# One stream of score turns over all query blocks, with one extra turn per block for left keys and denominators

## The chip, the cores and the metric

The kernel runs on one core of a Trainium2 chip. The metric is the device time of one execution in microseconds (us). The kernel before was run three times: 3818.97 us median, 3816.32 to 3819.16.

## What is computed

The whole kernel is a chain of four layers over a tensor of 4 images, 56 x 56 pixels, 128 channels. Only the first layer matters here. It takes each image as 3136 tokens, applies attention in windows and then attention over all tokens of the image, and then a multilayer perceptron. The change is in the attention over all tokens, which is called once per image:

```python
q = (x @ wq + bq).reshape(n, s, NH, dk).transpose(0, 2, 1, 3)     # NH = 4 heads, dk = 32, s = 3136 tokens
...
scores = jnp.einsum('nhqd,nhkd->nhqk', q, k) / jnp.sqrt(jnp.float32(dk))
attn = jax.nn.softmax(scores, axis=-1)
out = jnp.einsum('nhqk,nhkd->nhqd', attn, v)
out = out.transpose(0, 2, 1, 3).reshape(n, s, c)
return out @ wo + bo
```

All data are 32-bit floats. The scores are small enough that no maximum is subtracted: the kernel takes exp of the scaled scores, sums the values with these weights, and divides by the sum of the weights.

## The kernel before

`fast_attention` (L572) first calls `fast_windows`, which leaves queries and keys transposed in `qT` and `kT` (128 partitions: 4 heads of 32 rows; 3136 columns) and the values in `va` (25 chunks of keys). The attention itself then runs over seven blocks `j` of 448 queries (NB = 448, NBLK = 7).

For one block the 3136 keys are 24 whole chunks `c` of 128 keys and 64 left keys (chunk 24). A **slot** is the score of one chunk and one head, 128 keys x 448 queries, and fills one bank of PSUM. So a block has 96 slots. Slots are handled in half turns. `bank(turn)` gives either four banks (`s0`) or three (`s1`), in alternation by the counter `n`; the eighth bank is `po`, in which the values add up. One half turn is up to four or three score matmuls on TensorE (PE; L661), and one exp on ScalarE (ACT; L663) that moves all these banks into consecutive slots of `ring` in SBUF. The ring has RING = 28 slots, seven chunks. A half turn is cut where the ring ends and where the block's 96 slots end (L657).

Three things read a chunk in the ring. `sums` (L603) adds chunks 0 to 21 into `acc` on VectorE (DVE; L606), 21 additions per block. `values` (L608) multiplies the chunk with the values into `po` (PE; L612), four matmuls, one per head. For chunks 22 and 23, which DVE does not add, `finish` multiplies by ones (L620), so that PE sums over keys; `acc` is multiplied by ones too, as the sum over the 128 partitions is still open.

After the 96 slots of a block comes a half turn for the left keys: scores (L673), exp into `p24` (L676). Work that reads exps is put into a list `late` with the turn from which it may run, and `flush` runs it after every second half turn. So values come some two half turns behind their exps, then `raw`, the copy of `po` to SBUF (L647, ACT), and then `finish` (L614): the denominators by ones into a bank (L620, L623), the output projection of the block before (L626), one copy of both to SBUF (L628, ACT), reciprocal (L629, DVE), product with `raw` (L630) and, for the block before, the addition to `xf` (L635). `finish` takes a half turn of its own. The last block's projection is L684.

The order on PE is that of the program (`manual_schedule`). The order on ACT and DVE in this stage is chosen by the scheduler of the language.

Of the kernel before, what the change touches and what calls it, by code (L numbers as in the profile page):

```python
# [12 lines left out]
F32 = mybir.dt.float32  # L13
AF = mybir.ActivationFunctionType
ALU = mybir.AluOpType
# [4 lines left out]
P = 128  # L20
B = 4
HH = 56
TOK = HH * HH
NB = 448
NBLK = TOK // NB
# [15 lines left out]
def blk(j):  # L41
    return slice(j * NB, (j + 1) * NB)
# [523 lines left out]


RING = 28
SUMMED = 22


def fast_attention(k, w, xw, xf, beside, mr):  # L572

    nc, tc = k.nc, k.tc
    scale = 1.0 / math.sqrt(32.0)
    heads = [slice(32 * h, 32 * h + 32) for h in range(4)]  # L580
    half = (slice(0, 64), slice(64, 128))
    with ExitStack() as es:
        big = es.enter_context(tc.tile_pool(name="f_big", bufs=1))
        qT = big.tile([P, TOK], F32, name="f_qT")
        kT = big.tile([P, TOK], F32, name="f_kT")
        va = big.tile([P, 25, P], F32, name="f_va")
        fast_windows(k, w, xw, xf, mr, beside, qT, kT, va)

        ring = es.enter_context(tc.tile_pool(name="f_ring", bufs=1)).tile([P, RING, NB], F32, name="f_ring")
        wk = es.enter_context(tc.tile_pool(name="f_wk", bufs=2))  # L590
        ps = es.enter_context(tc.tile_pool(name="f_ps", bufs=1, space=PSUM))
        oT = es.enter_context(tc.tile_pool(name="f_out", bufs=1)).tile([P, TOK], F32, name="f_oT")
        late = []
        n = 0

        def bank(turn):
            return ps.tile([P, (4, 3)[turn], 512], F32, tag="s%d" % turn, name="f_s%d" % turn)

        def slots(j, c):
            s = (96 * j + 4 * c) % RING  # L600
            return ring[:, s:s + 4, :]

        def sums(j, c, acc):  # L603

            if 0 < c < SUMMED:
                nc.vector.tensor_add(acc, slots(j, 0) if c == 1 else acc, slots(j, c))  # L606

        def values(j, c, po, p24):  # L608
            for h in range(4):
                o = half[h % 2] if c == 24 else slice(0, P)  # L610
                p = p24[o, h // 2, :] if c == 24 else slots(j, c)[:, h, :]
                nc.tensor.matmul(po[heads[h], :NB], va[o, c, heads[h]], p, start=(c == 0), stop=(c == 24))  # L612

        def finish(j, raw, acc, p24, pd):  # L614


            for c in range(SUMMED - 1, 24):
                p = acc if c < SUMMED else slots(j, c)
                for h in range(4):
                    nc.tensor.matmul(pd[heads[h], 0, :NB], k.ones[:, 0:32], p[:, h, :], start=(c < SUMMED), stop=False)  # L620
            for h in range(4):
                o = half[h % 2]
                nc.tensor.matmul(pd[heads[h], 0, :NB], k.ones[o, 0:32], p24[o, h // 2, :], start=False, stop=True)  # L623
            m = 1 + (j > 0)
            if j:
                nc.tensor.matmul(pd[:, 1, :NB], w.wo, oT[:, blk(j - 1)], start=True, stop=True)  # L626
            den = wk.tile([P, 2, NB], F32, name="f_den")
            nc.scalar.copy(den[:, :m], pd[:, :m, :NB])  # L628
            nc.vector.reciprocal(den[:, 0], den[:, 0])  # L629
            nc.vector.tensor_mul(oT[:, blk(j)], raw, den[:, 0])  # L630
# [6 lines left out]
        def flush(all_=False):  # L637

            nonlocal n
            if n % 2 and not all_:  # L640
                return
            while late and (all_ or late[0][0] < n):
                _, f, *a = late.pop(0)
                if f is finish:
                    a.append(bank(n % 2))
                    n += 1
                f(*a)  # L647

        with tc.manual_schedule(engines={mybir.EngineType.PE}):
            for j in range(NBLK):  # L650
                po = ps.tile([P, 512], F32, tag="po", name="f_po")
                raw = wk.tile([P, NB], F32, name="f_raw")
                acc = wk.tile([P, 4, NB], F32, name="f_acc")
                t, done = 0, 0
                while t < 96:
                    turn, slot = n % 2, (96 * j + t) % RING
                    m = min((4, 3)[turn], RING - slot, 96 - t)  # L657
                    ss = bank(turn)
                    for i in range(m):
                        c, h = divmod(t + i, 4)  # L660
                        nc.tensor.matmul(ss[:, i, :NB], kT[heads[h], c * P:(c + 1) * P], qT[heads[h], blk(j)],  # L661
                                         start=True, stop=True)
                    nc.scalar.activation(ring[:, slot:slot + m, :], ss[:, :m, :NB], AF.Exp, scale=scale)  # L663
                    t += m
                    while 4 * (done + 1) <= t:
                        sums(j, done, acc)
                        late.append((n + 2, values, j, done, po, None))
                        done += 1
                    n += 1
                    flush()  # L670
                ss = bank(n % 2)
                for h in range(4):
                    nc.tensor.matmul(ss[half[h % 2], h // 2, :NB], kT[heads[h], 24 * P:TOK], qT[heads[h], blk(j)],  # L673
                                     start=True, stop=True)
                p24 = wk.tile([P, 2, NB], F32, name="f_p24")
                nc.scalar.activation(p24, ss[:, 0:2, :NB], AF.Exp, scale=scale)  # L676
                late.append((n + 2, values, j, 24, po, p24))
                late.append((n + 2, nc.scalar.copy, raw, po[:, :NB]))
                late.append((n + 3, finish, j, raw, acc, p24))
                n += 1  # L680
                flush()
            flush(True)
# [1097 lines left out]
class Plan:  # L1780
# [655 lines left out]
def build(k, packs, I, out):  # L2436
# [3 lines left out]
    with ExitStack() as es:  # L2440
# [15 lines left out]
        with tc.tile_pool(name="w01", bufs=1) as wp, tc.tile_pool(name="io", bufs=1) as io:  # L2456
# [129 lines left out]
```

## Time and profile before

| what | before |
|---|---|
| median of three runs | 3818.97 us (3816.32 to 3819.16) |
| span of the profiled execution | 3813.2 us |
| the same, from first score to last projection, per image | 381.7, 381.7, 381.6, 382.8 us |
| PE busy in the span | 3506.3 us |
| DVE busy in the span | 2895.7 us |
| ACT busy in the span | 2076.4 us |
| exps of score slots (L663) | 796 |
| additions of chunks on DVE (L606) | 588 |

The profiled execution's own time is known by its span, from the first to the last instruction; the median of the runs is 5.8 us longer, which is what lies around the span. A busy time counts an engine once where instructions overlap. Each matmul of 32-bit floats has two records in the profile, so 2688 score matmuls appear as 5376. In a row of the timeline stand the start in us from the begin of the span, the length, the engine, the line, the operation, what is written and read, and in brackets the idle time of the engine ahead of it and what ended that.

### The profile page before, as it was taken

How to read it: one execution, taken by the hardware profiler on the slowest of the kernel's cores; microseconds unless marked ns; L12 is line 12 of the kernel's file. 1: busy time of each engine (PE TensorE's matmuls, PEld its weight loads, DVE VectorE, ACT ScalarE, POOL GpSimd, SP SyncE). 2: the span in 40 equal slices, each digit the busy share in tenths (PEclk: the TensorE clock that was granted, in tenths of full speed). 3: DMA queues.
4: the chain of work that ended last, by engine and by line, in shares of the span. 5: the costliest groups of instructions: out<-in, count | busy, mean ns of one | idle time of the engine just before them, and what ended most of it. 6: DMA issues, size and time to landing. Idle time of an engine off the chain costs nothing. (4 is left out here: it accounts for less than half of the span.)

```text
span 3813.2 us, 79448 instructions
## 1 busy us (share of the span) xinstructions
PE 3506.3 (92%) x35416; PEld 1559.0 (41%) x35416; DVE 2895.7 (76%) x2703; ACT 2076.4 (54%) x2080; POOL 1210.5 (32%) x667
## 2 busy tenths in 40 slices
PE   6899999989999898899999989998998889998998
PEld 4322234553222455322244552222456533335665
DVE  6588877858888787688878758888796666775676
ACT  4577765448777455577755448776553111213452
POOL 0000006600000372000016600000474768994677
PEclk8999999999999999999999999999998989999999
DMA  2000000000000000000000000000002036862011
GB/s 97 1 1 1 1 1 19 19 18 1 1 1 1 18 3 19 18 1 1 1 1 19 19 18 1 1 1 1 35 3 87 6 67 146 175 145 81 35 49 51
DMA packets 73497, 111.13 MB, mean 29 GB/s; under 512 B 62140, under 2 KB 63932, under 8 KB 67900
## 3 DMA queue, kind: packets, MB, share of 16 engines
q1 hardware_dynamic: 14460, 93.13, 8.2%
q10 hardware_dynamic: 58688, 12.85, 2.0%
q8 instruction: 280, 4.59, 0.5%
q14 instruction: 69, 0.57, 0.0%
HBM read 79.46 MB, written 26.51 MB: 28 GB/s over the span
## 5 line engine op out<-in xcount | busy, mean ns | idle before, releaser
L663 ACT ACTIVATE f_ring<-f_s 128x1792 f32<-128x1792 f32 (+3 forms) x796 | 1097.3, 1429 | 226.7 <-PE f_s L661 224.8
L606 DVE TENSOR_TENSOR f_acc<-f_acc,f_ring 128x1792 f32<-128x1792 f32 x560 | 1134.0, 2025 | 64.3 <-ACT f_ring L663 7.5
L661 PE MATMUL f_s<-f_qT,f_kT 32*128 32x448 f32 x5376 | 738.1, 571 | 48.0 <-ACT f_ring L663 29.0
L877 POOL TENSOR_TENSOR m_sq<-m_y 128x392 f32<-128x392 f32 x16 | 14.5, 919 | 1973.8 <-ACT m_y L876 1973.7
L612 PE MATMUL f_po<-f_ring,f_va 128*32 128x448 f32 x5376 | 589.7, 546 | 0.0
L1029 DVE TENSOR_TENSOR e_td<-e_pa,e_c 128x1792 f32<-128x1792 f32 x252 | 491.4, 2015 | 14.3 <-ACT e_a L994 14.3
L1031 POOL TENSOR_TENSOR e_tp<-e_a,e_c 128x1792 f32<-128x1792 f32 x140 | 451.8, 3259 | 145.2 <-PE e_acc L1036 104.4
L661 PEld LDWEIGHTS f_s<-f_qT,f_kT 32*128 32x128 f32 x5376 | 268.0, 183 | 525.0 <-ACT f_ring L663 379.3
L1036 PE MATMUL e_acc<-e_td,t_shared 32*32 32x448 f32 x8064 | 323.8, 546 | 22.3 <-DVE e_td L1029 11.2
L1033 ACT ACTIVATE e_tp<-e_tp 128x1792 f32<-128x1792 f32 x140 | 235.1, 1697 | 176.5 <-POOL e_tp L1031 176.5
L1645 DVE TENSOR_TENSOR u_ud<-u_px,u_d 112x1792 f32<-112x1792 f32 x144 | 240.1, 1708 | 96.4 <-PE u_po L1650 87.3
L612 PEld LDWEIGHTS f_po<-f_ring,f_va 128*32 128x32 f32 x5376 | 132.8, 108 | 396.7 <-issue 395.7
L1036 PE MATMUL e_acc<-e_tp,t_shared 32*32 32x448 f32 x4480 | 222.3, 547 | 3.2 <-ACT e_tp L1033 2.5
L1650 PE MATMUL u_po<-u_ud,AT 112*64 112x448 f32 x960 | 201.5, 549 | 23.4 <-DVE u_ud L1645 23.4
L1647 POOL TENSOR_TENSOR u_up<-xh,u_d 112x1792 f32<-112x1792 f32 x64 | 193.7, 3053 | 25.8 <-PE u_po L1650 12.4
L1036 PEld LDWEIGHTS e_acc<-e_td,t_shared 32*32 32x32 f32 x8064 | 134.0, 103 | 146.8 <-DVE e_td L1029 56.1
L629 DVE RECIPROCAL f_den<-f_den 128x448 f32<-128x448 f32 x28 | 82.7, 2953 | 77.2 <-ACT f_den L628 77.2
L1650 PE MATMUL u_po<-u_up,AT 112*64 112x448 f32 x576 | 127.0, 548 | 0.1
L1650 PEld LDWEIGHTS u_po<-u_ud,AT 112*64 112x64 f32 x960 | 64.9, 137 | 148.0 <-issue 86.7
L606 DVE TENSOR_TENSOR f_acc<-f_ring 128x1792 f32<-128x1792 f32 x28 | 56.7, 2024 | 86.6 <-ACT f_ring L663 57.8
L1512 POOL TENSOR_TENSOR q_u<-iS,q_g 128x1792 f32<-128x1792 f32 x32 | 102.8, 3236 | 55.8 <-PE s_px L1360 32.9
L1036 PEld LDWEIGHTS e_acc<-e_tp,t_shared 32*32 32x32 f32 x4480 | 95.1, 103 | 55.4 <-ACT e_tp L1033 19.3
(485 smaller groups left out, 4727.3 us busy)
## 6 DMA issues: line engine op xcount, KB each, us to landing
u_d<-dd SPq DMA_DIRECT2D x48, 784.0 KB
xw<-in_x SPq DMA_DIRECT2D x4, 1568.0 KB
x2d<-x SPq DMA_DIRECT2D x4, 1568.0 KB
xad<-x SPq DMA_DIRECT2D x4, 1568.0 KB
x_xs<-xad ACTq DMA_DIRECT2D x32, 196.0 KB
xm<-x_ev ACTq DMA_DIRECT2D x64, 98.0 KB
o_a<-xm SPq DMA_DIRECT2D x8, 784.0 KB
o_x<-x2d SPq DMA_DIRECT2D x4, 1568.0 KB
```

The lines of the kernel that those rows point to most:

```text
L606: nc.vector.tensor_add(acc, slots(j, 0) if c == 1 else acc, slots(j, c))
L612: nc.tensor.matmul(po[heads[h], :NB], va[o, c, heads[h]], p, start=(c == 0), stop=(c == 24))
L661: nc.tensor.matmul(ss[:, i, :NB], kT[heads[h], c * P:(c + 1) * P], qT[heads[h], blk(j)], start=True, stop=True)
L663: nc.scalar.activation(ring[:, slot:slot + m, :], ss[:, :m, :NB], AF.Exp, scale=scale)
L1029: nc.vector.tensor_tensor(t, am, cm, ALU.max)
L1031: nc.gpsimd.tensor_sub(t, bc(a.rearrange("p (l n) -> p l n", l=8), 1, 4), cm)
L1033: nc.scalar.activation(tf, tf, AF.Relu)
L1036: nc.tensor.matmul(acc[quarters[q], r, :NB], k.ident[o, o], t[o, q].rearrange("p l n -> p (l n)"), start=(g == 0), stop=(g == len(EDGE_TUR ...
L1512: nc.gpsimd.tensor_mul(u, bc(st.iS[:, bp, c, :HH], 1, HEADS), bc(g[:, n, c, :], 2, HH))
L1645: nc.vector.tensor_mul(u, bc(px[:, :, :NB], 2, m), dm)
L1647: nc.gpsimd.tensor_mul(u, bc(x, 2, m), dm)
L1650: nc.tensor.matmul(po[64 * b2:64 * b2 + 64, :NB], st.AT[:, 8 * i + h0 + q, 2 * bp + b2, :], u[:, b2, q, :], start=(left == 16), stop=(left ...
```

## The change

The score slots of all seven blocks become one stream of 672 slots in 96 turns. Every turn has a half turn of four slots and one of three; a turn may hold the end of one block and the begin of the next. `slots` stays as it was, since it already counted through the blocks. A list `queue` takes the chunks whose exps a turn has issued; `values()` runs what is in `ready` and then moves the queue there, so that values come one turn behind. It stops after a block's chunk 23, when `raw` is copied out of `po`, and leaves what follows for the next call.

The turn after a block's first slot (`ends`, with AFTER = 1: turns 0, 14, 28, 42, 55, 69 and 83) is followed by an extra turn: the left keys of the block that has just begun (`remainder`, in the four banks), a second call of `values()`, and the denominators of the block that has just ended (`finish`, in the three banks). The values of the left keys (chunk 24) come with the next turn's chunks, in the middle of the sum, and chunk 23 is the last.

ACT and DVE are issued in the order of the program in this stage too. DVE adds chunks 0 to 21 as before, and 0 to 20 in the last block, where PE takes 21 with 22 and 23. `BY_DMA` is empty, so the branches with a DMA are never taken.

```diff
-SUMMED = 22
+TURN = 7
+BY_DMA = ()
+BY_ONES = (22, 23)
+LAST_ONES = (21, 22, 23)
+AFTER = 1
...
+        def value(j, c):
+            e = blocks[j]
+            if c == 0:
+                e.po = ps.tile([P, 512], F32, tag="po", name="f_po")
             for h in range(4):
                 o = half[h % 2] if c == 24 else slice(0, P)
+                p = e.p24[o, h // 2, :] if c == 24 else slots(j, c)[:, h, :]
+                nc.tensor.matmul(e.po[heads[h], :NB], va[o, c, heads[h]], p, start=(c == 0), stop=(c == 23))
+            if c == 23:
+                e.raw = wk.tile([P, NB], F32, name="f_raw")
+                nc.scalar.copy(e.raw, e.po[:, :NB])
+
+        def values():
+
+            while ready:
+                j, c = ready.pop(0)
+                value(j, c)
+                if c == 23:
+                    break
+            ready.extend(queue)
+            queue.clear()
+
+        def remainder(j):
+            ss = bank(0)
+            for h in range(4):
+                nc.tensor.matmul(ss[half[h % 2], h // 2, :NB], kT[heads[h], 24 * P:TOK], qT[heads[h], blk(j)],
+                                 start=True, stop=True)
+            blocks[j].p24 = wk.tile([P, 2, NB], F32, name="f_p24")
+            nc.scalar.activation(blocks[j].p24, ss[:, 0:2, :NB], AF.Exp, scale=scale)
+
+        def finish(j):
+
+            e = blocks[j]
+            pd = bank(1)
+            for n, p in enumerate([e.acc] + [slots(j, c) for c in by_ones(j)]):
...
-        with tc.manual_schedule(engines={mybir.EngineType.PE}):
...
+        with tc.manual_schedule(engines={mybir.EngineType.PE, mybir.EngineType.Activation, mybir.EngineType.DVE}):
+            t = 0
+            ends = {-(-96 * j // TURN) - 1 + AFTER: j for j in range(NBLK)}
+            for turn in range(96 * NBLK // TURN):
+                for half_turn in range(2):
+                    m = (4, 3)[half_turn]
+                    ss = bank(half_turn)
                     for i in range(m):
+                        j, c = divmod((t + i) // 4, 24)
+                        h = (t + i) % 4
                         nc.tensor.matmul(ss[:, i, :NB], kT[heads[h], c * P:(c + 1) * P], qT[heads[h], blk(j)],
                                          start=True, stop=True)
+                    slot = t % RING
                     nc.scalar.activation(ring[:, slot:slot + m, :], ss[:, :m, :NB], AF.Exp, scale=scale)
+                    for q in range(t // 4, (t + m) // 4):
+                        queue.append(divmod(q, 24))
+                        add(*divmod(q, 24))
                     t += m
+                values()
+                if turn in ends:
+                    j = ends[turn]
+                    remainder(j)
+                    values()
+                    if j:
+                        finish(j - 1)
+                    queue.append((j, 24))
+            while ready or queue:
+                values()
+            finish(NBLK - 1)
```

In the rest of `finish` the matmuls by ones, the projection, the copy, the reciprocal, the product and the addition to `xf` are as before, with `e.p24` and `e.raw` in the places of `p24` and `raw`.

More of the change, by code (lines that the diff above doesn't have):

```diff
@@ L592, in fast_attention, with by_ones @@
         oT = es.enter_context(tc.tile_pool(name="f_out", bufs=1)).tile([P, TOK], F32, name="f_oT")
-        late = []
-        n = 0
+        blocks = [Env() for _ in range(NBLK)]
+        queue, ready = [], []
+        def by_ones(j):
+            return LAST_ONES if j == NBLK - 1 else BY_ONES
         def bank(turn):
@@ L601, in slots, with add @@
             return ring[:, s:s + 4, :]
[L603 to L608, printed above, removed]
+        def add(j, c):
+            e = blocks[j]
+            if c in by_ones(j):
+                return
+            if c in BY_DMA:
+                if c == BY_DMA[0]:
+                    e.far = wk.tile([P, 4, NB], F32, name="f_far", bufs=1)
+                    nc.sync.dma_start(e.far, slots(j, c))
+                else:
+                    nc.gpsimd.dma_start(e.far, slots(j, c), accum_op=ALU.add)
+                return
+            if c == 0:
+                return
+            if not hasattr(e, "acc"):
+                e.acc = wk.tile([P, 4, NB], F32, name="f_acc")
+                nc.vector.tensor_add(e.acc, slots(j, 0), slots(j, c))
+                return
+            if BY_DMA and c == last_add(j):
+                nc.vector.tensor_add(e.acc, e.acc, e.far)
+            nc.vector.tensor_add(e.acc, e.acc, slots(j, c))
@@ L609, in values, with last_add @@
+        def last_add(j):
+            return max(c for c in range(24) if c not in BY_DMA and c not in by_ones(j))
+        def value(j, c):
+            e = blocks[j]
+            if c == 0:
+                e.po = ps.tile([P, 512], F32, tag="po", name="f_po")
             for h in range(4):
                 o = half[h % 2] if c == 24 else slice(0, P)
-                p = p24[o, h // 2, :] if c == 24 else slots(j, c)[:, h, :]
-                nc.tensor.matmul(po[heads[h], :NB], va[o, c, heads[h]], p, start=(c == 0), stop=(c == 24))
@@ L614, in finish @@
-        def finish(j, raw, acc, p24, pd):
-            for c in range(SUMMED - 1, 24):
-                p = acc if c < SUMMED else slots(j, c)
+                p = e.p24[o, h // 2, :] if c == 24 else slots(j, c)[:, h, :]
[11 more added lines that the diff above has]
+            queue.clear()
@@ new lines, in remainder @@
+        def remainder(j):
[6 more added lines that the diff above has]
+        def finish(j):
+            e = blocks[j]
+            pd = bank(1)
+            for n, p in enumerate([e.acc] + [slots(j, c) for c in by_ones(j)]):
@@ L619, in finish @@
                 for h in range(4):
-                    nc.tensor.matmul(pd[heads[h], 0, :NB], k.ones[:, 0:32], p[:, h, :], start=(c < SUMMED), stop=False)
+                    nc.tensor.matmul(pd[heads[h], 0, :NB], k.ones[:, 0:32], p[:, h, :], start=(n == 0), stop=False)
             for h in range(4):
                 o = half[h % 2]
-                nc.tensor.matmul(pd[heads[h], 0, :NB], k.ones[o, 0:32], p24[o, h // 2, :], start=False, stop=True)
+                nc.tensor.matmul(pd[heads[h], 0, :NB], k.ones[o, 0:32], e.p24[o, h // 2, :], start=False, stop=True)
@@ L629, in finish @@
             nc.vector.reciprocal(den[:, 0], den[:, 0])
-            nc.vector.tensor_mul(oT[:, blk(j)], raw, den[:, 0])
+            nc.vector.tensor_mul(oT[:, blk(j)], e.raw, den[:, 0])
             if j:
@@ L635, in output @@
             nc.vector.scalar_tensor_tensor(xf[:, blk(j)], pm, w.fbvo, xf[:, blk(j)], ALU.add, ALU.add)
[L637 to L647, printed above, removed]
-        with tc.manual_schedule(engines={mybir.EngineType.PE}):
[L650 to L658, printed above, removed]
+        with tc.manual_schedule(engines={mybir.EngineType.PE, mybir.EngineType.Activation, mybir.EngineType.DVE}):
[5 more added lines that the diff above has]
+                    ss = bank(half_turn)
@@ L659, in fast_attention @@
                     for i in range(m):
-                        c, h = divmod(t + i, 4)
+                        j, c = divmod((t + i) // 4, 24)
+                        h = (t + i) % 4
                         nc.tensor.matmul(ss[:, i, :NB], kT[heads[h], c * P:(c + 1) * P], qT[heads[h], blk(j)],
                                          start=True, stop=True)
+                    slot = t % RING
                     nc.scalar.activation(ring[:, slot:slot + m, :], ss[:, :m, :NB], AF.Exp, scale=scale)
+                    for q in range(t // 4, (t + m) // 4):
+                        queue.append(divmod(q, 24))
+                        add(*divmod(q, 24))
@@ L664, in fast_attention @@
                     t += m
[L665 to L682, printed above, removed]
+                values()
[6 more added lines that the diff above has]
+                    queue.append((j, 24))
```

## Prediction

> **What bounds the kernel now.** The page comes first, for the engines and the groups that the change touches.
>
> ```profile
> PE 3506.3 (92%) x35416; PEld 1559.0 (41%) x35416; DVE 2895.7 (76%) x2703; ACT 2076.4 (54%) x2080; POOL 1210.5 (32%) x667
> ...
> L663 ACT ACTIVATE f_ring<-f_s 128x1792 f32<-128x1792 f32 (+3 forms) x796 | 1097.3, 1429 | 226.7 <-PE f_s L661 224.8
> L606 DVE TENSOR_TENSOR f_acc<-f_acc,f_ring 128x1792 f32<-128x1792 f32 x560 | 1134.0, 2025 | 64.3 <-ACT f_ring L663 7.5
> L661 PE MATMUL f_s<-f_qT,f_kT 32*128 32x448 f32 x5376 | 738.1, 571 | 48.0 <-ACT f_ring L663 29.0
> ```
>
> The second look is the busy table of four windows, each from an image's first score to its last projection (L684). The columns are window, length, then busy time of PE, PEld, DVE, ACT and POOL.
>
> ```profile
> 151.60:533.30 381.70, 360.88 (x3037) 110.64 (x3037) 324.88 (x167) 292.38 (x223) 0.00 (x0) 1.00 0.00 1
> 861.20:1242.90 381.70, 360.91 (x3037) 110.66 (x3037) 324.86 (x167) 292.42 (x223) 0.00 (x0) 1.00 0.00 1
> 1571.10:1952.70 381.60, 360.85 (x3036) 110.54 (x3036) 324.87 (x167) 292.39 (x223) 0.00 (x0) 1.00 0.00 1
> 2284.50:2667.30 382.80, 360.93 (x3036) 109.94 (x3036) 324.89 (x167) 292.64 (x223) 0.00 (x0) 1.00 0.00 1
> ```
>
> The stage takes 4 x 382 us, 40% of the span. PE is busy 361 of 382; DVE at 325 is second, ACT at 292 third. Third comes the timeline: one whole turn inside a block, then the turn of a block.
>
> ```profile
> 343.45 1.78 PE L661 MATMUL f_s<-f_qT,f_kT 32*128 32x448 f32 x14
> 344.55 2.85 ACT L663 ACTIVATE f_ring<-f_s 128x1792 f32<-128x1792 f32 x2 [0.94 <-PE f_s L661]
> 345.16 1.71 PE L612 MATMUL f_po<-f_ring,f_va 128*32 128x448 f32 x16
> ...
> 346.80 1.78 PE L661 MATMUL f_s<-f_qT,f_kT 32*128 32x448 f32 x14
> ...
> 356.74 0.98 PE L673 MATMUL f_s<-f_qT,f_kT 32*64 32x448 f32 x8
> ...
> 361.95 0.96 PE L612 MATMUL f_po<-f_p,f_va 64*32 64x448 f32 x8
> 363.07 0.96 PE L620 MATMUL f_s<-f_acc,c_ones 128*32 128x448 f32 x8 [0.17 <-ACT f_ring L663]
> ...
> 367.40 0.91 ACT L628 COPY f_den<-f_s 128x896 f32<-128x896 f32 x1 [3.52 <-PE f_s L626]
> 368.34 2.95 DVE L629 RECIPROCAL f_den<-f_den 128x448 f32<-128x448 f32 x1 [2.83 <-ACT f_den L628]
> ```
>
> Inside a block PE is back to back: seven score slots and two value chunks in 3.35 us, ACT waiting for PE. A turn with one value chunk is limited by the loop score, exp, score instead and takes 2.82 (at 336.85 and 339.67), the turn after it 3.78. Four turns hold seven chunks: 3.35 + 3.35 + 2.82 + 3.78 = 13.30 us, 3.325 a turn. A block of 96 slots is 96/7 = 13.71 turns, 45.6 us. The seven remainders (L673) of image 0 start at 198.56, 250.10, 303.67, 356.74, 410.88, 464.01 and 518.09: 53.26 us a block. So **7.66 us a block** go to the rest: the left keys, their values, the denominators, and turns cut short at the ring's end and the block's end.
>
> [...] I read PE from starts in the timeline, not from the 92%. [...] 14 records of 0.57 us on average end in 1.78 us, and rounds of four follow each other at 0.376 us. [...] the trace has 1.66 and 1.29, overlap 0.10. [...]
>
> **The change part by part.**
>
> *Turns.* Removed is the cut of turns. The ring of 28 is four times 7, so a stream of 4 and 3 never meets its end. Half turns per image before: 199 exps (796/4), 7 remainders, 7 denominators, 213. After: 192 + 14 = 206. The exps of L663 fall from 796 to 768. At a full half turn (1.67 us) this would be 7 x 1.67 = 11.7 us an image. But a short turn costs PE less than a full one, and the gain must be set against what the extra turn loses.
>
> *The extra turn.* I followed the new order, starting each piece when its engine is free and what it reads ended 0.055 us ago (the gap that the trace shows between an exp and the scores waiting for it); durations are those of the rows, with 0.54 for the copy of raw (L647), 0.92 for the left keys' exp (L676) and 0.91 for the denominators' copy (L628). Turn 28, from its first score: scores 0 and 0.86, exps 1.11 to 2.77 and 2.67 to 3.95, values of the old block's last chunk at 1.71. The remainder needs bank 0: 2.83. ACT copies raw behind both exps, 3.85 to 4.39, then exps the remainder until 5.20. The second call of values takes chunks 0 and 1, exps of this same turn; it needs the one accumulator bank and starts at 4.44, **PE standing 0.70**. Two chunks (1.64) bring 6.08. The denominators are 8 rounds of 0.376 plus 0.27 and the projection 0.95: 10.31. ACT's copy runs 10.47 to 11.37. Turn 29: four scores at 10.31, three must wait for bank 1 until 11.43, exps until 13.08 and 14.26; the list of values is empty. Turn 30: scores wait for these exps, 13.14 and 14.32; then three chunks (left keys, 2, 3) from 15.28 to 17.81. Three ordinary turns with five whole chunks take 3.35 + 2.82 + 3.78 = 9.95, so the extra turn costs **7.85 us**: 5.98 of its own PE work (0.91 + 0.84 + 4.23) and 1.87 of standing. The other five alignments give, from extra turn to extra turn, 53.7, 53.9, 51.8, 53.7 and 54.4 us for 69 turns: 267.5 - 69 x 3.325 = 38.1, **7.6 us a block**. Before it was 7.66.
>
> *DVE and ACT in program order.* The adds remain 21 a block (20 in an image's last block: 2.13 less for DVE there, 0.75 more for PE). DVE reaches the denominators' reciprocal at 5.3 and gets its input at 11.4, about 6 us idle; before it idled some 5 (2.83 for the copy, 1.8 ahead of the first add). It then follows 20 adds at 2.13 us, while chunks come every 1.90: it falls behind, and PE's finish finds the sum ready by 1.1 to 3.1 us. Ring slots come free 4 us before they are needed. Both are hidden by these margins, nothing else. Nothing in the stage runs on POOL or a DMA queue that is moved.
>
> *Ends.* Lead-in: turn 0 has a remainder too, and turn 14 starts at 49.9 (14 x 3.325 = 46.6, and 3.3 of filling and first table load). Then 267.5. From turn 83 to the final projection 64.2: 47.8 to turn 95 (17.8 for the extra turn's three, then nine of 3.33), and from there DVE's last add (6.8), finish with one more chunk (5.1), copy, reciprocal and product (4.5). Total **381.5 us an image**. The same rule on the old order gives 382.3 where the trace has 381.7. The difference by one rule is -0.7, against the trace itself -0.1; times four, -0.5 to -3 us. I take -3: the profile's 3813.2 goes to 3810. The span is 5.8 below the median of the runs, which holds what lies around it: 3819.0 - 3 = **3816**. The 28 extra turns each have waits that no trace shows; at +-0.3 us each that is +-8, so 3808 to 3825 for this case.
>
> **The rivals.** About 0.2% (7.6 us) is what a measurement can tell from no change.
>
> *The bubbles close* (0.18). If the extra turn costs only its 5.98 us, each of 24 interior blocks gains 1.7 and the stage 41: 3778. For it: seven half turns fewer per image, ACT free for 90 us of each. Against: the one accumulator bank, and two turns with 0 and 3 chunks in place of 2 and 2, come from the order itself.
>
> *DVE takes over* (0.22), the case on the slower side. Place: the first matmul of finish, which waits for the last add. It decides from 1.1 us of lateness at the tightest block on. Twenty adds at 2.23 instead of 2.13 would be 2 us late; with 1.5 us of it seen by PE in 24 blocks, 36 us: 3852. For it: DVE idles a microsecond longer per block, in fixed order behind the reciprocal. Against: adds measure 2.025 and start 2.13 apart with no wait, and the page counts only 7.5 us of waiting for exps.
>
> *The change does not do what it says*: turns still cut. Excluded by 28 = 4 x 7; the count of L663 would show it.
>
> *No change* (0.60) is the forecast: two orders with the same rounds, the same adds, and 7.6 against 7.66 us of loss. Range: to leave out no more than 2 in 10, half of each rival: 3793 to 3842; the likeliest case alone 3808 to 3825. Faster 0.18, same 0.60, slower 0.22.
>
> **What would show it.** L663's exps 768, in two forms of 384; ordinary turns still 3.35 us; about 10.3 us from the extra turn's first score to the next turn's, then 2.8 and 4.7; extra turns 51.8 to 54.4 us apart; stage 381 to 382. PE waiting for L606 at the denominators in every block would be the DVE rival; extra turns 51.5 us apart on average the fast one. If the extra turn's three windows differ from 17.8 by over a microsecond, my prediction is wrong in its main step.

## Result and profile after

The kernel after took 3829.23 us (median of six runs, 3826.52 to 3830.47), beside 3817.64 us for the kernel before in runs of the same time (3814.45 to 3819.25): ratio 1.0026, 95% interval 1.0015 to 1.0038. It is slower by 11.6 us. The forecast was 3816, no change. The profiled spans are 3827.2 us after and 3813.2 before, 14.0 apart. A run's time exceeds its span by 1.7 to 2.1 us in every execution on record. So of the 5.8 us that were taken for what lies around the span, some 4 are that the profiled execution of before was faster than the median; and the 14.0 are a little more than the medians differ.

First the same parts of the page as before: the engines, the exps, the additions, the scores. The last line is the reciprocal of the denominators; the figure behind its last bar is DVE's idle time ahead of it.

```profile
PE 3493.9 (91%) x35448; PEld 1560.1 (41%) x35448; DVE 2892.5 (76%) x2699; ACT 2069.8 (54%) x2052; POOL 1209.3 (32%) x667
...
L701 ACT ACTIVATE f_ring<-f_s 128x1792 f32<-128x1792 f32 (+1 forms) x768 | 1091.2, 1475 | 193.9 <-PE f_s L698 191.0
L630 DVE TENSOR_TENSOR f_acc<-f_acc,f_ring 128x1792 f32<-128x1792 f32 x556 | 1125.7, 2025 | 56.8 <-ACT f_ring L701 1.4
L698 PE MATMUL f_s<-f_qT,f_kT 32*128 32x448 f32 x5376 | 718.2, 571 | 54.7 <-ACT f_ring L701 28.2
...
L680 DVE RECIPROCAL f_den<-f_den 128x448 f32<-128x448 f32 x28 | 82.7, 2953 | 138.8 <-ACT f_den L679 138.8
```

The change does what it says: 768 exps in two forms instead of 796 in four, 556 + 28 additions instead of 588, and 32 records of matmuls more (one chunk more by ones in each image's last block: 4 images x 4 heads x 2 records). DVE waits 62 us more ahead of its 28 reciprocals (138.8, before 77.2), 2.2 us each.

Then the busy table, one window per image from its first score to its last projection (now L718), the columns as before:

```profile
151.00:531.80 380.80, 356.03 (x3045) 110.14 (x3045) 322.94 (x166) 290.54 (x216) 0.00 (x0) 1.00 0.00 1
860.00:1240.80 380.80, 356.07 (x3045) 110.13 (x3045) 322.89 (x166) 290.54 (x216) 0.00 (x0) 1.00 0.00 1
1569.60:1953.60 384.00, 358.98 (x3044) 110.48 (x3045) 322.93 (x166) 290.61 (x216) 0.00 (x0) 0.99 0.00 1
2283.60:2665.40 381.80, 356.10 (x3045) 108.92 (x3045) 322.92 (x166) 291.07 (x216) 0.00 (x0) 1.00 0.00 1
```

The attention did not become slower. Three of four images take 0.9 to 1.1 us less than before. The last projection starts at 2665.40; before it started at 2667.34. At that point the kernel after is 1.9 us ahead. From there to the end of the span it needs 3827.2 - 2665.4 = **1161.8 us**, the kernel before 3813.2 - 2667.3 = **1145.9 us**. The loss of 15.9 us lies in code that the diff does not touch, and so not in the first layer, which alone was said to matter here.

Going on in the timeline of after, TensorE first. These are its rows in the spectra of the second layer, some 220 us after the last projection:

```profile
2883.02 6.69 PE L1356 MATMUL s_pr<-t_images,s_x 128*64 128x33 f32 x223 [1.00 <-DVE x L1043]
2892.81 0.19 PE L1356 MATMUL s_pr<-t_images,s_x 128*64 128x33 f32 x1 [3.10 <-issue]
...
2906.03 1.83 PE L1394 MATMUL s_px<-t_images,s_z 128*112 128x112 f32 x16
2924.20 0.58 PE L1284 MATMUL s_pt<-s_mv,t_shared 128*128 128x1 f32 x2 [16.34 <-DVE s_mv L1281]
```

The same rows of before:

```profile
2884.76 6.73 PE L1322 MATMUL s_pr<-t_images,s_x 128*64 128x33 f32 x224 [1.05 <-DVE x L1009]
...
2903.04 1.83 PE L1360 MATMUL s_px<-t_images,s_z 128*112 128x112 f32 x16
2908.02 0.38 PE L1250 MATMUL s_pt<-s_mv,t_shared 128*128 128x1 f32 x2 [3.16 <-DVE s_mv L1247]
```

Two waits are new. In the first transform PE does 223 of 224 records of matmuls and stands 3.10 us ahead of the last, for nothing that the profile shows ("issue"). Later it waits 16.34 us for `s_mv` from DVE, where it waited 3.16. Measured from the last projection, the matmul with `s_mv` comes at 258.8 us after and 240.7 us before, 18.1 later; 15.9 of that is left at the end. Behind its waits PE is also slower. Over the 20 us from the transform's first matmul the granted clock, as a share of TensorE's full clock, was 0.91 (before 1.00), and over the next 40 us 0.61 (before 0.74). How much of the 15.9 us that makes was not separated.

What DVE does meanwhile, in the timeline of after, with POOL's rows at the two moments that count:

```profile
2907.42 0.87 DVE L1784 TENSOR_TENSOR t_w_M<-t_w_M,t_w_M0rev 112x1 f32<-112x1 f32 x1
2907.65 1.40 POOL L1438 TENSOR_SCALAR d_m<-t_w_V,t_images 128x448 f32<-128x448 f32 x1
2908.99 3.82 DVE L1785 TENSOR_TENSOR t_w_M<-t_w_M,t_w_M0rev 112x1 f32<-112x1 f32 x1
2912.73 11.39 DVE L1787 TENSOR_SCALAR t_w_M<-t_w_M 112x62 f32<-112x62 f32 x1
...
2922.95 1.12 POOL L1451 TENSOR_TENSOR d_d<-d_d,d_t 128x448 f32<-128x448 f32 x1
2924.16 1.70 POOL L1450 TENSOR_SCALAR d_t<-t_w_V,t_images 128x448 f32<-128x448 f32 x1
```

And of before:

```profile
2904.43 0.14 DVE L1750 TENSOR_TENSOR t_w_M<-t_w_M,t_w_M0rev 112x1 f32<-112x1 f32 x1
2905.69 0.60 DVE L1751 TENSOR_TENSOR t_w_M<-t_w_M,t_w_M0rev 112x1 f32<-112x1 f32 x1
2906.21 0.18 DVE L1753 TENSOR_SCALAR t_w_M<-t_w_M 112x62 f32<-112x62 f32 x1
...
2908.28 1.40 POOL L1404 TENSOR_SCALAR d_m<-t_w_V,t_images 128x448 f32<-128x448 f32 x1
```

The three operations are small steps on weights of the third layer (`conv_weights`). They take 0.14, 0.60 and 0.18 us before, and 0.87, 3.82 and 11.39 after. On DVE the statistics `s_mv` stand right behind them. In before they end 1.9 us ahead of the large POOL operation `d_m` (2906.39 to 2908.28). In after DVE reaches them 4.9 us later, counted from the last projection, and meets POOL's run of large operations of `value_weights` and `score_weights`. In before DVE meets that run too, with later operations, and eleven of them take half a microsecond or more longer than alone. But they take only 0.9 to 1.5 us each, and none overlaps more than two instructions of POOL. That run has 17 POOL instructions in the 11.39 us, and its first pause is from 2924.07 to 2924.16. DVE's operation ends at 2924.12, in that pause. The hold of 3.82 us ended without a pause of POOL.

So the theory has two steps. **First**, PE's instructions come in packets, and where one packet ends has moved. The page's queue table has 280 instruction packets of 4.59 MB in all on queue q8, 16.4 KB each. PE has 71,238 records in the trace: 35,448 of matmuls, as many of weight loads, and 342 of its sequencer. If q8 carries PE's instructions, that is 254 records a packet. That it does is inferred, and the author's estimate for a packet is 256, which is also how far apart the two records lie at which PE waits in the runs below (58,112 and 58,368). Counting PE's records from 0 at the start of the trace, the matmul that waited is number 58,368 = 228 x 256. In the kernel before, that number falls 40 records behind the transform's last, and PE, which first waits 0.73 us for DVE there, shows no wait for its instructions. The change makes it 40 records earlier: 64 more of matmuls and weights, 24 fewer of the sequencer. **Second**, the delay puts DVE's small operations in step with POOL's run, which holds them.

The rivals: that the new order of attention leaves something behind (DVE or a transfer later than before); and that POOL's run is no cause, but a thing that stands beside it.

### The profile page after: what moved, and what is told of

It reads as the page before. It is cut to its first block, busy times and chain, and to the rows that moved or that the text cites. A ratio compares the mean times of both kernels' runs of the same rounds, so it can differ in the third digit from the quotient of the medians.

```text
span 3827.2 us, 79464 instructions
## 1 busy us (share of the span) xinstructions
PE 3493.9 (91%) x35448; PEld 1560.1 (41%) x35448; DVE 2892.5 (76%) x2699; ACT 2069.8 (54%) x2052; POOL 1209.3 (32%) x667
## 3 DMA queue, kind: packets, MB, share of 16 engines
q8 instruction: 280, 4.59, 0.5%
## 5 line engine op out<-in xcount | busy, mean ns | idle before, releaser
L701 ACT ACTIVATE f_ring<-f_s 128x1792 f32<-128x1792 f32 (+1 forms) x768 | 1091.2, 1475 | 193.9 <-PE f_s L698 191.0
L698 PE MATMUL f_s<-f_qT,f_kT 32*128 32x448 f32 x5376 | 718.2, 571 | 54.7 <-ACT f_ring L701 28.2
L698 PEld LDWEIGHTS f_s<-f_qT,f_kT 32*128 32x128 f32 x5376 | 258.6, 183 | 520.5 <-ACT f_ring L701 387.6
L680 DVE RECIPROCAL f_den<-f_den 128x448 f32<-128x448 f32 x28 | 82.7, 2953 | 138.8 <-ACT f_den L679 138.8
L1546 POOL TENSOR_TENSOR q_u<-iS,q_g 128x1792 f32<-128x1792 f32 x32 | 102.8, 3239 | 72.5 <-PE s_px L1394 49.9
L891 ACT ACTIVATE m_hT<-m_ph,w_fb 128x392 f32<-128x392 f32 x128 | 72.8, 589 | 70.3 <-PE m_ph L890 64.9
```

## Experiments

The table collects all runs. "Rest" is the profiled time from the last projection to the end of the span. Rest, waits and hold are each of one profiled execution. Each ratio is to the kernel before in runs of the same time, whose medians were 3817.64 us (beside after), 3820.05 (the runs with 10 and 54 matmuls, `t_w_M` on POOL, one call), 3820.50 (the late weights with `d_`, and one call + 47) and 3821.43 (the runs without `d_`, and + 64 matmuls); so medians of different lines compare to some 4 us only. "PE waits" are the waits of over 0.5 us without a shown cause in the first transform of the spectra or just behind it; "hold" is the longest of DVE's operations on single columns or weights of up to 384 elements there, which take 0.1 to 0.4 us when nothing holds them.

| kernel | median us | ratio to before, 95% | rest us | PE waits us | hold us |
|---|---|---|---|---|---|
| before | 3817.64 | | 1145.9 | none | 1.23 |
| after | 3829.23 | 1.0026 (1.0015 to 1.0038) | 1161.8 | 3.10 | 11.39 |
| before + 10 matmuls | 3829.28 | 1.0025 (1.0016 to 1.0033) | 1160.8 | 2.44 | 11.38 |
| before + 64 matmuls | 3819.11 | 0.9997 (0.9988 to 1.0005) | 1146.1 | none | 1.24 |
| after + 54 matmuls | 3819.17 | 0.9995 (0.9987 to 1.0003) | 1146.8 | none | 1.63 |
| after, `t_w_M` on POOL | 3824.87 | 1.0010 (1.0004 to 1.0017) | 1157.1 | 3.12 | 7.94 |
| after, conv weights late | 3829.89 | 1.0026 (1.0016 to 1.0036) | 1165.5 | 2.52 | 3.96 |
| after, without `d_` operations | 3820.85 | 1.0001 (0.9992 to 1.0009) | 1155.1 | 3.98, 1.35 | 0.35 |
| one call | 3790.34 | 0.9924 (0.9911 to 0.9936) | 1160.5 | 0.71, 2.84 | 7.07 |
| one call, late | 3789.60 | 0.9921 (0.9908 to 0.9935) | 1160.3 | 1.47 | 4.50 |
| one call + 47 matmuls | 3772.19 | 0.9879 (0.9864 to 0.9894) | 1145.4 | none | 1.23 |
| the same, late | 3792.66 | 0.9925 (0.9911 to 0.9938) | 1160.3 | none | 7.73 |
| the same, late, without `d_` | 3787.96 | 0.9913 (0.9900 to 0.9927) | 1156.1 | 3.16, 3.04 | 0.22; 3.15 at the weights' new place |

The rest takes one of two sizes, 1145 to 1147 or 1155 to 1166, whatever the attention is.

### The packet's end alone, in the kernel before

Ten matmuls of one column (two records of matmul and two of weights each, so 40 records) ahead of the last image's final projection. The attention is the old one.

```diff
+PADS = [0, 0, 0, 10]
...
-        pm = ps.tile([P, 512], F32, tag="po", name="f_pf")
+            pm = ps.tile([P, 512], F32, tag="po", name="f_pf")
+            for _ in range(PADS.pop(0)):
+                nc.tensor.matmul(pm[0:32, 500:501], k.ones[:, 0:32], oT[:, 0:1], start=True, stop=True)
```

> The kernel before, with ten one-column matmuls (40 records on PE) ahead of the last image's final projection, where PE waits about 5 us for DVE anyway. They write a column of PSUM that nobody reads. Theory A (where PE's instruction stream is cut): in the changed kernel PE has issued 41 records more than before when the spectra begin (57922 against 57881), and there PE stands 3.1 us ahead of the last matmul of L1356 with nothing to wait for but its own instructions; DVE then meets POOL's run of additions and is held some 15 us. With 40 records more the kernel before has the cut at the same place: PE stands about 3 us there, and the run takes about 3828 to 3832, that is 10 to 14 us more than before. Theory B (the order on ACT and DVE, or the data's place, is the cause): 3818, unchanged within 3 us.

The kernel before, with 0.9 us of work added on PE, takes 3829.28 us, 9.2 more than the kernel before beside it: by the ratios the same loss. (The first transform starts at record 57,922 in after and 57,882 in before, 40 apart, not the 41 of the expectation.) The timeline of this kernel, PE and DVE:

```profile
2898.86 2.19 PE L1341 MATMUL s_ps<-s_z,t_images 128*128 128x56 f32 x6 [2.44 <-issue]
...
2918.59 11.38 DVE L1756 TENSOR_SCALAR t_w_M<-t_w_M 112x62 f32<-112x62 f32 x1
```

The wait stands just behind the transform, at record 58,369, one from the multiple of 256, and the same operation is held as long as in after. The new attention is not needed for the loss.

### A whole packet more, in the kernel before

The same edit with 16 matmuls per image: 64, or 256 records, the estimate for a packet.

```diff
+PADS = [16, 16, 16, 16]
```

> The kernel before with 64 one-column matmuls (16 ahead of each image's final projection), 256 records of PE more[...], so the cuts between packets fall where they fell before. The theory (where the cut falls decides) expects no wait of 2 us in the first transform or the inverse transform, the operations on t_w_M under 1 us, and no more than the matmuls' own time: 3818 to 3825. The rival, that more instructions on PE are late as such, expects more than ten matmuls gave: 3829 or above, with PE's wait of 2 to 3 us.

3819.11 us, no difference, with over six times as many matmuls added as in the run that lost 9 us. PE waits nowhere in the transform, the holds are those of before. More instructions as such cost nothing here; what matters is where the multiples of 256 fall. This was not varied finely: the kernels without `d_` aside, PE waits where the transform starts 65 to 90 records behind a multiple, and does not where it starts 18 to 26 behind.

### The packet's end put back, in the kernel after

```diff
+PADS = [14, 14, 13, 13]
```

> The changed kernel, with 54 one-column matmuls (216 records on PE) spread as 14, 14, 13, 13 over the waits ahead of the four final projections. 41 + 216 = 257[...], so the cuts of PE's stream stand in the spectra as they do in the kernel before. Theory A: PE's wait of 3.1 us ahead of the last matmul of the first transform is gone, DVE isn't held for 11 us at t_w_M, and the run takes 3812 to 3818, some 13 us less than the changed kernel's 3829. Theory B: 3829 and more, up to 4 us for the matmuls where they stick out of the wait.

The 257 of the expectation is one more than the 256 records estimated for a packet. The run took 3819.17 us, ratio 0.9995: the loss is gone, by adding work. The timeline has 224 matmuls without a wait, and DVE passes:

```profile
2888.65 6.73 PE L1359 MATMUL s_pr<-t_images,s_x 128*64 128x33 f32 x224 [1.00 <-DVE x L1046]
...
2909.61 1.63 DVE L1788 TENSOR_TENSOR t_w_M<-t_w_M,t_w_M0rev 112x1 f32<-112x1 f32 x1
2911.16 0.18 DVE L1790 TENSOR_SCALAR t_w_M<-t_w_M 112x62 f32<-112x62 f32 x1
```

With the rest as it was, the change is what the prediction said of it, no change.

### The held operations taken from DVE

The operations on `t_w_M` go to POOL.

```diff
-        nc.vector.tensor_add(m[:, 0, 0:1], m[:, 0, 0:1], rev[:, 0:1])
-        nc.vector.tensor_sub(m[:, 1, 0:1], m[:, 1, 0:1], rev[:, 1:2])
-        nc.vector.tensor_scalar_mul(m[:, :, 0], m[:, :, 0], 0.5)
-        nc.vector.tensor_scalar_mul(m[:, :, 1:], m[:, :, 1:], math.sqrt(2.0))
+        nc.gpsimd.tensor_add(m[:, 0, 0:1], m[:, 0, 0:1], rev[:, 0:1])
+        nc.gpsimd.tensor_sub(m[:, 1, 0:1], m[:, 1, 0:1], rev[:, 1:2])
+        nc.gpsimd.tensor_scalar_mul(m[:, :, 0], m[:, :, 0], 0.5)
+        nc.gpsimd.tensor_scalar_mul(m[:, :, 1:], m[:, :, 1:], math.sqrt(2.0))
```

> The changed kernel, with the eight small operations of conv_weights on t_w_M issued on POOL instead of DVE. Theory A: what costs most is DVE held behind POOL at three of these operations (0.9 + 3.8 + 11.4 us where before they took 0.9 in all). On POOL they can't be held by POOL: 3815 to 3820, 9 to 14 us less than the changed kernel; PE's wait of 3.1 us at the first transform stays. Rival C (DVE is held by whatever operation comes there[...]): the additions, squares and factors behind them are held instead, 3825 to 3829.

3824.87 us, between the theory and its rival: some 4 us of the 12 by the medians, 6 by the ratios, and 4.7 in the rest. DVE's next weights take the place of those moved (timeline of this kernel):

```profile
2909.00 4.30 DVE L1789 TENSOR_SCALAR t_w_W<-t_w_W 128x384 f32<-128x384 f32 x1
...
2914.01 7.94 DVE L1791 TENSOR_SCALAR Wr<-t_w_W 128x384 f32<-128x384 f32 x1
```

So it is not the operation itself that is slow: what comes in its place at that time is held.

In another kernel all of these weights (`conv_weights`, except what needs the slot pool) are issued at the end of `spectra`, behind the statistics.

```diff
+        conv_weights(k, w, st.conv)
...
-def conv_weights(k, w, pool, late):
+def conv_weights(k, w, pool):
...
+def conv_slots(k, w, pool, late):
```

> The changed kernel, with all of conv_weights but its last tile (slot) issued on DVE at the end of the spectra, behind their last copies, instead of in their middle, where POOL adds without a pause. PE's instructions are as in the changed kernel, so its wait of 3.1 us at the first transform stays. Theory A (the first loss is PE's wait, the larger one DVE held behind POOL at these operations): DVE reaches the aggregate (s_mv) without being held, 10 to 13 us come back and up to 3 go for the operations at their new place: 3817 to 3822. Rival C (whatever comes on DVE is held as long): 3826 to 3830.

No gain, 3829.89 us, as the rival had it. `s_mv` itself is free (1.67 us at 2909.37), but the next operation on single columns, `s_t` at L1289, is held 3.96 us, `s_d` at L1300 2.60, and at their new place several of the moved weights are held some 3 us each. Of the expected gain 6.3 us come, and go again. The last `s_px` matmul (L1394) ahead of the matmuls on `q_u` is that much sooner than in after, counted from the last projection (311.2 us, 317.5). Then the first matmul on `q_u`, which DVE makes behind these weights, waits 12.14 us where it waited 3.3.

### POOL's run taken away

```diff
-    half = wk.tile([32, 2, HH], F32, name="d_half")
...
     f = wk.tile([P, 3, 8, HH], F32, name="d_f")
-    for ri in range(2):
-        nc.gpsimd.tensor_scalar_mul(t, w.V[:, ri], w.pvh[:, 0:1])
...
+    nc.gpsimd.memset(f, 0.0)
```

> The changed kernel with the products and sums of value_weights (d_half to d_f, 18 operations on POOL) left out: d_f is set to zero, so the second layer's values are left out of what it computes. What the same engine does beside it, the q_ operations of score_weights, stays. If DVE is held by POOL's gapless run (theory), that run ends some 10 us earlier: PE still stands 3 us in the first transform, since nothing changes for its instruction packets, but the DVE operation that took 11.39 us takes under 4, s_mv comes some 10 us sooner, and the time is 3814 to 3821. If DVE was held by something else that comes with PE's wait (its own instructions late, a transfer), taking POOL's work away changes only what waits for POOL: 3826 to 3831, and the operation still takes over 8 us.

3820.85 us, inside the theory's range, ratio 1.0001. (Seventeen operations are left out, not 18.) In the timeline the same operation of 112x62 takes 0.19 us, and no weight takes over 0.35:

```profile
2906.51 0.35 DVE L1771 TENSOR_SCALAR Wr<-t_w_W 128x384 f32<-128x384 f32 x1
2906.78 0.16 DVE L1766 TENSOR_SCALAR t_w_M<-t_w_M 112x2 f32<-112x2 f32 x1
2906.84 0.19 DVE L1767 TENSOR_SCALAR t_w_M<-t_w_M 112x62 f32<-112x62 f32 x1
```

POOL's other operations there, the `q_` ones, now end at 2897.67, where in after they run to 2922.97, and DVE's small ones come in another order. So the edit moved more than it took away. What it shows is that with POOL idle nothing on DVE is held: POOL's run is what holds it. But `s_mv` came only 5.8 us sooner than in after, not 10 (its matmul on PE 253.0 us from the last projection, against 258.8), since PE stood at other places:

```profile
2891.15 5.23 PE L1356 MATMUL s_pr<-t_images,s_x 128*64 128x33 f32 x95 [3.98 <-issue]
2897.73 5.55 PE L1356 MATMUL s_pr<-t_images,s_x 128*64 128x33 f32 x129 [1.35 <-issue]
```

The second wait is at a multiple of 256 (58,112). The first, 3.98 us ahead of the transform's first matmul, is at none (57,922); what it waits for is open, though there too an instruction packet that set off late, 7.5 us behind the one before it, had ended 1.8 us earlier. With no hold on DVE at all, the rest of this execution is still 9 us over that of before, and over the 20 us from the transform's first matmul the granted clock was 0.59. That points to a price of PE's waits by themselves. But the profiled execution was one of the slowest of 13 (3827.44 us), and by the ratio no loss is left; how large that price is stays open.

### One call of values in the extra turn

The prediction's rival "the bubbles close" named what speaks against it: the accumulator bank, and two turns with 0 and 3 chunks. Both come from the second `values()` in the extra turn. Without it the list of values is left to the next turn.

```diff
                     remainder(j)
-                    values()
                     if j:
                         finish(j - 1)
```

> The changed kernel without the second call of values() in the extra turn, so the chunks of that turn come with the next turn's, whose list was empty. Forecast by the rule of the prediction: turn 28 to turn 31 in 16.8 us instead of 17.8, extra turns 52.5, 52.3, 50.2, 52.4 and 52.8 us apart instead of 53.7, 53.9, 51.8, 53.7 and 54.4, and 371.3 us an image instead of 381.5: 41 us less than the changed kernel, 3786 to 3792, as the places where PE's instructions are cut stay. Rival D (DVE takes over, since denominators then start 2 us earlier than the last addition allows): PE waits for L630 in every block and 375 to 381 us an image, 3803 to 3829.

3790.34 us, 0.8% faster than before. The stage takes 372.0, 371.9, 372.2 and 373.7 us; the turns that an extra turn follows start 52.2, 52.2, 50.2, 52.3 and 52.7 us apart, 1.4 less than in after on average. The turn of a block in the timeline, whose extra turn has no values:

```profile
313.23 0.98 PE L660 MATMUL f_s<-f_qT,f_kT 32*64 32x448 f32 x8
...
314.35 0.96 PE L671 MATMUL f_s<-f_acc,c_ones 128*32 128x448 f32 x8
...
318.58 2.09 PE L698 MATMUL f_s<-f_qT,f_kT 32*128 32x448 f32 x14
...
320.60 2.46 PE L642 MATMUL f_po<-f_ring,f_va 128*32 128x448 f32 x24
...
322.99 1.78 PE L698 MATMUL f_s<-f_qT,f_kT 32*128 32x448 f32 x14
```

The values of the next turn now fill the time in which ACT exps that turn's scores. The denominators start 1.1 us behind the remainder's scores; for the same turn in after it is 3.7. PE's waits for DVE's sums there are four, 3.2 us in all, so the prediction's rival "DVE takes over" does not come true even with less cover. The rest of this kernel is still 1160.5, with PE's waits at 58,112 and at 58,368, both multiples of 256.

### One call, and the packet's end

The same with 12, 12, 12 and 11 matmuls of one column, which put the packet's end near where it lies in before.

```diff
-                    values()
...
+PADS = [12, 12, 12, 11]
```

> The kernel with one call of values() in the extra turn, plus 47 one-column matmuls (188 records) ahead of the four final projections. At the first transform of the spectra PE has then issued 57943 + 188 records, 19 beyond a multiple of 256, as in the changed kernel with 54 such matmuls (19) and nearly as before (23); without them it is 87, and PE stood 0.7 and 2.8 us there and DVE 13 us. Theory A: both are gone, 3776 to 3781, 10 to 14 us less than without the matmuls (3790). Theory B (the place of the cut mattered by chance in two kernels): 3790.

**3772.19 us**, ratio 0.9879, the fastest of all. The rest is 1145.4 us, and nothing is given back. The four stages are 1489.2 us together, before 1527.9: 38.7 of the 44.2 us between the spans. Of the other 5.5, 0.4 lie behind the last projection and 4.3 between the third and the fourth image, a stretch that differs by as much among profiles with the same code there (327.4 to 331.8 us).

The late weights were put into the kernel with one call too, without and with these matmuls:

> The kernel with one call of values() in the extra turn, and conv_weights at the end of the spectra. Theory A: 9 to 13 us less than the 3790 of one call alone, since DVE is no longer held behind POOL, while PE's waits of 0.7 and 2.8 us stay: 3778 to 3782. Rival C: 3788 to 3791.

> One call of values(), 47 one-column matmuls and conv_weights at the end of the spectra. If PE's wait only costs because DVE then meets POOL, the two remedies don't add: 3775 to 3781, within 2 us of the better of the two alone. If PE's wait costs its own 3 us besides, this is 2 to 4 us better than conv_weights moved alone.

3789.60 us, no gain again; and 3792.66, a **loss of 20 us** against the version with the weights at their old place. The first is in its rival's range, the second a miss. In the second PE does not stand in the transform, yet DVE is held.

```profile
2870.71 3.50 DVE L1291 TENSOR_TENSOR s_t<-s_mv,s_mr 128x1 f32<-128x1 f32 x1
2874.24 7.73 DVE L1292 SCALAR_TENSOR_TENSOR s_t<-s_t,s_mv 128x1 f32<-128x1 f32 x1
```

So PE's wait is one way to bring DVE into POOL's run; another order on DVE is a second. By the last `s_px` matmul this kernel is 6.8 us behind the one with the weights at their old place (309.0 us from the last projection, 302.2); 8.8 more come at the weights' new place (below).

> One call of values in the extra turn, 47 more one-column matmuls, and the weights of the third layer's convolution late (the version that took 3792.66), with the same 18 operations of value_weights on POOL left out (the second layer's values are left out of what it computes). Theory: with the late weights DVE meets POOL's run in another operation (7.73 us at L1292); without that run nothing holds it, and the time falls by 12 to 22, to 3771 to 3781. If the late order itself costs time on DVE or PE, the time stays above 3786.

3787.96 us: 5 us of the 12 to 22, a miss. DVE is free up to the weights' new place, but PE stands 3.16 us ahead of the transform and 3.04 us at record 58,368, although the count of its instructions is that of the run with no wait. So the place of a packet's end alone does not tell whether PE waits. That the packet must also be late is the author's reading, and what would have made it late in this kernel, which has other work and transfers on POOL's side, was not shown.

But the two waits are not what keeps the time up. The last `s_px` matmul comes 302.8 us from the last projection, in before 302.5. The late order does it. PE's first matmuls on `q_u`, in before and in this kernel (timelines):

```profile
2973.42 2.00 PE L1527 MATMUL q_acc<-q_u,S 64*64 64x448 f32 x12 [3.30 <-DVE q_u L1514]
2945.22 2.54 PE L1544 MATMUL q_acc<-q_u,S 64*64 64x448 f32 x12 [12.14 <-DVE q_u L1531]
```

In all four kernels with late weights this wait is 12.1 us, in all others 3.3. On DVE the weights stand ahead of `q_u` there, beside POOL's own `q_u` operations of some 3.2 us, and three of them take 3.15, 3.05 and 3.23 us. The 8.8 us are most of the 10.3 by which this kernel's rest is longer than that of before.

## Why the prediction was wrong

**The stage was right.** Its working holds to 0.2 us, from part to part. Turn 28 of image 0, timeline of after, PE and ACT:

```profile
254.45 1.78 PE L698 MATMUL f_s<-f_qT,f_kT 32*128 32x448 f32 x14
...
257.27 0.98 PE L660 MATMUL f_s<-f_qT,f_kT 32*64 32x448 f32 x8
258.28 0.54 ACT L645 COPY f_raw<-f_po 128x448 f32<-128x448 f32 x1
...
258.87 1.71 PE L642 MATMUL f_po<-f_ring,f_va 128*32 128x448 f32 x16 [0.62 <-ACT f_raw L645]
...
264.60 2.09 PE L698 MATMUL f_s<-f_qT,f_kT 32*128 32x448 f32 x14
264.71 0.91 ACT L679 COPY f_den<-f_s 128x896 f32<-128x896 f32 x1 [5.07 <-PE f_s L677]
265.65 2.95 DVE L680 RECIPROCAL f_den<-f_den 128x448 f32<-128x448 f32 x1 [6.38 <-ACT f_den L679]
...
267.42 2.21 PE L698 MATMUL f_s<-f_qT,f_kT 32*128 32x448 f32 x14 [0.72 <-ACT f_ring L701]
...
272.08 1.78 PE L698 MATMUL f_s<-f_qT,f_kT 32*128 32x448 f32 x14
```

From the turn's first score: remainder 2.82 (forecast 2.83), copy of `raw` 3.83 (3.85), second call of values 4.42 (4.44) with PE standing 0.62 (0.70), next turn 10.15 (10.31), the one after 12.97 (13.14), end of its values 17.63 (17.81). DVE idles 6.38 us ahead of the reciprocal (about 6). The two times that the prediction takes for exps, 1.66 us for four slots and 1.29 for three, are 1.67 and 1.29 in after, and neighbours overlap by 0.10. That the copy of `raw` waits for both exps ahead of it was assumed: it starts at 258.28, and they run from 255.55 to 258.40. Turn 14, the second that an extra turn follows, starts 49.8 us into the stage (49.9), the later ones 53.6, 53.8, 51.6, 53.5 and 54.2 us apart (53.7, 53.9, 51.8, 53.7, 54.4), and 64.2 us follow (64.2). The stage is 380.7 us in the first two images (381.5). DVE did not take over: PE waits for the sums (L671) four times, in the last block of each image, 7.9 us in all.

**What failed is the last term of the sum.** The prediction took the difference of the stage times four and put it on the whole time: "the profile's 3813.2 goes to 3810". That holds only if the 1145.9 us behind the last projection stay as they are, and this was nowhere argued. The prediction looked for what else could change among engines and queues inside the stage ("Nothing in the stage runs on POOL or a DMA queue that is moved"), and did not count the instructions of PE, though the page lists 280 instruction packets on a queue of their own (q8). The rest measured 1161.8, so this term was zero in the sum and is +15.9 between the two profiles. The stage's own term was -3; the four images come to 1527.2 us against 1527.9, -0.7, and would be -3.9 but for image 2, which took 3.2 us more than the first two (below).

**The ranges.** The bounds of the likeliest case, 3808 to 3825, came from the 28 extra turns alone, and missed by 4 us; none of the rivals had its place outside the stage. That the whole range, 3793 to 3842, holds 3829 is luck: it reaches so far only for the sake of the DVE rival. The rival on the slower side (DVE, at the first matmul of `finish`) did not happen. The fast rival's price of 3778 was about right for a kernel that closes the bubbles, 3772 with one call and the packet's end in place, but the kernel as changed does not.

**What is shown and what is not.** Shown: the loss comes with the number of PE's instructions alone (before + 10), goes with it (after + 54), and returns to nothing with 256 records more (before + 64); POOL's run is what holds DVE (in the two kernels without the `d_` operations the longest of DVE's small operations there takes 0.35 and 0.22 us, where it takes 11.39 and 7.73 with them; nothing is held until POOL works again, at the weights' new place, where three take 3.05 to 3.23). That PE waits for a packet is inferred, from the records' numbers and from the packets' own records: each of the nine waits at 58,112 or 58,368 ended 1.2 to 1.6 us after the packet of queue q8 with the number 227 or 228, counted from 0. Which records a packet carries the trace does not tell, and the numbers do not match everywhere: in after, record 57,856 = 226 x 256 starts at 2875.78 us, before packet 226 sets off at 2879.77. Not shown: why one packet is late. In the traces of before, after, before + 10, before + 64 and one call + 47, one packet sets off 6.6 to 7.6 us after the one before it, towards the transform's end; its neighbours do so after 3.1 to 4.7 us, and in this transform PE uses up 256 records in 6.73 x 256 / 448 = 3.8 us. Large transfers run at the same time (88 and 87 GB/s from 2870 to 2965 us in before and after), but no run took them away. Not shown either: what lets a DVE operation in between two POOL instructions, as at 2906.21 in before, or keeps it out for 17; nor how the loss divides among PE's wait, its slower clock behind it and DVE's hold.

## What to carry to other kernels

Split a predicted span at the end of the changed stage and ask of the unchanged remainder what sets its timing: an engine's instruction count, and which engines meet there at what phase. If a small edit moves the time by a few tenths of a per cent, compare the two traces behind the edit first, and add a few idle instructions, then a whole packet's worth (here ten matmuls cost 9.2 us, and 64, or 256 records, nothing), before believing that the edit itself is slow or fast. Where DVE and POOL worked side by side here, free margin on DVE alone did not protect it: a small operation of 0.2 us that met POOL's run at another moment took 11. And when work is moved out of such a place, look at the new place too: there the late weights lost 8.8 us.

## What the runs showed of the hardware

At this place PE's waits without a shown cause fell mostly on one record in 256. Each such wait of over 0.5 us in or just behind the first transform, nine in all the traces here, stands at record 58,112 (227 x 256) or 58,368 (228 x 256), within one record. Two others stand ahead of the transform's first matmul, in the two kernels without the `d_` operations.

A short DVE operation was kept out over many POOL instructions. The operation of 112x62 that takes 0.18 us in before, and 0.19 without the `d_` operations, took 11.39 us in after. POOL ran 17 instructions in that time, the longest of 1.39 us, so the hold outlasted each of them, and it ended in a pause of 0.09 us. The hold of 3.82 us ahead of it ended without a pause. By what POOL's run holds DVE was not shown.

PE also ran at half its clock behind one wait, and not behind another of the same length. In images 1 and 2 of after, the remainder of turn 0 stands behind a wait of 2.44 us; its 8 records take 0.98 us in the one and 1.77 in the other (timeline of after):

```profile
864.23 0.98 PE L660 MATMUL f_s<-f_qT,f_kT 32*64 32x448 f32 x8 [2.44 <-ACT f_ring L701]
...
1573.91 1.77 PE L660 MATMUL f_s<-f_qT,f_kT 32*64 32x448 f32 x8 [2.44 <-ACT f_ring L701]
1575.60 1.58 PE L642 MATMUL f_po<-f_ring,f_va 128*32 128x448 f32 x8
```

From 1573.5 to 1576.9 us the granted clock was 0.50; from 864 to 868 us it was 1.00. A second such stretch, from 1942.1 to 1945.5 us, has 0.51. The two make up the 3.2 us of image 2, 1.2 in the first and 2.0 in the second. In before the granted clock was 1.00 in all four stages. So between single profiles an image's time can't be compared to better than some 3 us.
